# Four image layers in one Trainium2 kernel: layer 0's scores and products in runs of 6, 4, 6 and 4, 8, 4 units

## The chip, the cores and the metric

The kernel runs on one core of a Trainium2 chip. A core has a matrix engine (TensorE, PE in the profile), a vector engine (VectorE, DVE), a scalar engine (ScalarE, ACT), GpSimd (POOL) and DMA queues, of which SyncE (SP) issues most here. They run side by side[...]. The metric is the device time of one execution in microseconds (us); lower is better.

## The reference

The input is four images of 64 x 64 places with 64 channels, in float32. Four layers follow one another:

```python
# layer 0: attention over the N = 4096 places of an image
q, k, v = x @ Wq + bq, x @ Wk + bk, x @ Wv + bv
attn = softmax(q @ k.T, axis=-1)
x = gamma * (attn.T @ v) + x              # summed over the query place
# layer 1: LayerNorm, 64 -> 256, 3x3 depthwise convolution, two halves multiplied,
#          channel attention, 128 -> 64, added to x; LayerNorm, 64 -> 256,
#          two halves multiplied, 128 -> 64, added to x
# layer 2: self-attention between the 64 x 64 rows "b, c" of the image, on x itself
x = softmax(x @ x.T) @ x + x
# layer 3: attention with 32 inner channels, a projection to 64, BatchNorm over all images
f = softmax((x @ theta) @ (x @ phi).T, axis=-1)
wy = (f @ (x @ g)) @ W + b
x = x + batchnorm(wy)
```

In layer 0 the softmax runs over the keys j of a query i, and the product sums over i. So for each tile of 128 queries the kernel makes the scores against all keys, takes their exponential, and scales v of these queries by the reciprocal of the row sums; the product then adds this tile's part to all 4096 outputs.

## The kernel before, in words

**Layout.** `X` keeps the four images in SBUF, each as 128 partitions (two halves of the image by 64 channels) by 2048 places. PSUM is divided into three buffers `ps` of 128 x 1024 (scores, projections and all else) and two accumulators `acc` of 128 x 512. The exponentials go to six buffers `e` of 128 x 2048 in SBUF.

**Layer 0** has 32 tiles t of 128 queries an image. `scores(t)` has four parts g. Each part is four matmuls of 64 x 64 weights (four quarters of the array at once), which fill one `ps`, and one exponential on ScalarE with the row sums in `zs` (lines 1031 and 1036). I call a part a score unit. `scale(t)` on VectorE adds the four sums, takes the reciprocal and multiplies v into `vq` (lines 1045 to 1048). `products(p, half)` takes two tiles, 2p and 2p + 1, and half of the outputs: for each of the two tiles and two accumulators, two matmuls of 128 x 64 weights with `vq` as the weights (line 1056). I call these two matmuls a product unit. An accumulator that has both tiles is added to `y` on VectorE (line 1063). The profile counts each float32 matmul as two.

**The order** is written out by hand: PE, ScalarE and VectorE take their instructions as the program emits them. A list `items` holds one entry for each layer 0 tile (then for the steps of layers 2 and 3), and `due[i]` what comes after item i. Two lanes, `conv` and `misc`, hold generators of other work. The lane of `conv` runs layer 1 of image b beside layer 0 of image b + 1; its longest part is the depthwise convolution, nine taps for each of 4 x 2 blocks, every tap one VectorE instruction of 128 x 1024 (lines 1155 to 1160). The lane of `misc` turns and projects the images to come (`load_x`, `project0`). A generator yields the us that its step is to take, and `tick(us)` lets a lane catch up:

```python
fn()                                   # scores(t)
for lane in (conv, misc):
    lane.tick(us)                      # 3.6
for fn in due.get(i, []):              # products(p, half), then scale(t)
    fn()
for lane in (conv, misc):
    lane.tick(us)
```

So a round is four score units, lane work, four product units, the scale of that round's tile, lane work. In `due` the products were entered ahead of the scales, and products of tiles 2p and 2p + 1 begin in the round of tile 2p + 2.

**Other places that the change touches.** `fetch_x` loads image 0 in two halves; `setup` turns the small vectors and folds LayerNorm into `pw1` and `pw3`, in item 3 (lines 879 to 912); `project0` makes q with its bias on VectorE (line 990) and v; in layer 3, `products` adds exponentials on VectorE into `esum`, and `totals` turns the sums of a block of 32 steps into reciprocals with a logarithm, an exponential and a Newton step; `finish` makes the BatchNorm and stores, with `check_sums` ahead of the last copies.

Of the kernel before, what the change touches and what calls it, by code (L numbers as in the profile page):

```python
# [691 lines left out]
def fast_path(ctx: ExitStack, tc: tile.TileContext, a: dict, out: bass.AP, bad):  # L692
# [44 lines left out]

    def fetch_x(b, queues):
        if b % 2 == 0:
            fetch_x.both = new_big("xr")  # L740
        t = fetch_x.both[:, bass.ts(b % 2, 2048)].rearrange("p (q n) -> p q n", n=128)
        src = a["x"][b].rearrange(by_rows, p=2, q=16)
        for g in range(2):
            for p in range(2):
                (queues[p] if b == 0 else queues[g]).dma_start(
                    out=t[64 * p : 64 * p + 64, bass.ts(g, 8)], in_=src[p, :, bass.ts(g, 8)]
                )
        rows_x.append(t)
# [3 lines left out]
    nc.sync.dma_start(out=qk[:, 64:128], in_=a["L0_conv_Wk"])  # L752
    fetch_x(0, (nc.sync, nc.scalar))
    bq = const.tile([64, 1], F32, name="bq")
    nc.sync.dma_start(out=bq, in_=a["L0_conv_bq"].rearrange("(n o) -> n o", o=1))
# [123 lines left out]
    def setup():  # L879
        nc.vector.tensor_add(cmat, cmat, ident)  # L880
        ps = new_ps()
        nc.tensor.transpose(ps[:, 512 : 512 + n_rows], rows, ident[:n_rows, :n_rows])
        nc.vector.tensor_copy(vec, ps[:, 512 : 512 + n_rows])
        yield 5.0

        ps = new_ps()
        for i, (w_, sh, bi) in enumerate(
            ((pw1, "L1_conv_ln1_b", "L1_conv_pw1_b"), (pw3, "L1_conv_ln2_b", "L1_conv_pw3_b"))
        ):
            for r in range(2):  # L890
                mm(
                    ps[:, 2 * i + r : 2 * i + r + 1], w_[0:64, bass.ts(r, 128)], V(sh, 0, 0, 64),
                    start=True, stop=True,
                )
            nc.vector.tensor_add(
                pwb[:, i, :], ps[:, 2 * i : 2 * i + 2], vec[:, col[bi] : col[bi] + 2]
            )

        ps = new_ps()
        for i, (w_, g) in enumerate(((pw1, "L1_conv_ln1_g"), (pw3, "L1_conv_ln2_g"))):  # L900
            nc.vector.tensor_scalar_mul(w_, w_, V(g))
            mm(ps[:, 512 * i : 512 * i + 256], cmat, w_, start=True, stop=True)
            nc.vector.tensor_copy(w_, ps[:, 512 * i : 512 * i + 256])
        for i in range(4):
            nc.vector.tensor_scalar_mul(half[:, bass.ts(i, 64)], ident[:, 0:64], 0.5)
            stt(
                half[:, bass.ts(i, 64)], ident[:, 64:128], -0.5 if i > 1 else 0.5,
                half[:, bass.ts(i, 64)], ALU.mult, ALU.add,
            )
        nc.vector.tensor_mul(resb[:, 0:1], V("L1_conv_pw2_b"), V("L1_conv_beta"))  # L910
        nc.vector.tensor_mul(resb[:, 1:2], V("L1_conv_pw4_b"), V("L1_conv_gamma"))
        yield 3.0
# [7 lines left out]
    def load_x(b):  # L920
        for g in range(2):
            ps = new_ps()
            for i in range(8):
                nc.tensor.transpose(ps[:, bass.ts(i, 128)], rows_x[b][:, 8 * g + i, :], ident)
            (nc.vector.tensor_copy if g else nc.scalar.copy)(X[:, b, bass.ts(g, 1024)], ps)
            yield 3.0
# [44 lines left out]
    def project0(b):  # L971
# [5 lines left out]
        for j, w in once if b else ((0, "q"), (0, "v"), (1, "q"), (2, "q"), (1, "v"), (3, "q")):  # L977
            ps = new_ps()
            if w == "once":
# [7 lines left out]
                for o in range(2):  # L987
                    own, other = slice(64 * o, 64 * o + 64), slice(64 - 64 * o, 128 - 64 * o)
                    n = bass.ts(2 * j + o, 512)
                    nc.vector.tensor_scalar_add(  # L990
                        qs[own, :, n], ps[own, :].rearrange("p (s n) -> p s n", s=2), bqk[own, :]
# [26 lines left out]
    def layer0(b):  # L1018
        x, m, first = X[:, b], im[b], len(items)
        tiles = {}  # L1020

        def scores(t):
            es = [new_e() for _ in range(2)]
            zs = sm.tile([128, 4], F32, tag="zs", name="zs", bufs=4)
            vq = sm.tile([128, C], F32, tag="vq", name="vq", bufs=4)
            for g in range(4):
                ps = new_ps()
                for c in range(2):
                    for r in range(2):
                        rows_ = slice(64 * r, 64 * r + 64)  # L1030
                        mm(  # L1031
                            ps[64 * c : 64 * c + 64, bass.ts(r, 512)],
                            m.q[rows_, 128 * t + 64 * c : 128 * t + 64 * c + 64],
                            x[rows_, bass.ts(g, 512)], start=True, stop=True,
                        )
                act(  # L1036
                    es[g // 2][:, bass.ts(g % 2, 1024)], ps, AF.Exp, bias=SHIFT0,
                    accum_out=zs[:, g : g + 1],
                )
            tiles[t] = es, vq, zs  # L1040

        def scale(t):
            es, vq, zs = tiles[t]
            tot = sums0[:, b, t : t + 1]
            nc.vector.tensor_reduce(tot, zs, AX.X, ALU.add)
            rec = sm.tile([128, 1], F32, tag="rec", name="rec")
            nc.vector.reciprocal(rec, tot)
            nc.vector.tensor_scalar_mul(vq, m.v[:, t, :], rec)

        def products(p, half):  # L1050
            accs = [new_acc() for _ in range(2)]
            for t in (2 * p, 2 * p + 1):
                es, vq, _ = tiles[t]
                for g in range(2):
                    for r in range(2):
                        mm(  # L1056
                            accs[g][64 * r : 64 * r + 64, :], vq,
                            es[half][:, 1024 * g + 512 * r : 1024 * g + 512 * r + 512],
                            start=t == 2 * p, stop=t == 2 * p + 1,
                        )  # L1060
            for g in range(2):
                cols = bass.ts(2 * half + g, 512)
                stt(  # L1063
                    (x if p == 15 else m.y)[:, cols], accs[g], gam0,
                    (m.y if p else x)[:, cols], ALU.mult, ALU.add,
                )

        for t in range(32):
            items.append((lambda t=t: scores(t), 3.6))
        for p in range(16):  # L1070
            for half in range(2):
                at(first + 2 * p + 2 + half, lambda p=p, half=half: products(p, half))
        for t in range(32):
            at(first + t, lambda t=t: scale(t))
# [156 lines left out]
    def layer2(b):  # L1231
# [51 lines left out]
        for n in range(32):  # L1283
            items.append((lambda n=n: scores(n), 4.6))
            at(first + n + 1, lambda n=n: products(n))
# [3 lines left out]
    def close2(b):  # L1289
# [4 lines left out]
        for i in range(4):  # L1294
# [4 lines left out]
            yield 2.0 if i < 3 else 6.0  # L1299
# [3 lines left out]
    wys, early = {}, []  # L1303

# [44 lines left out]
    def layer3(b):  # L1349
# [3 lines left out]
        def scores(n):  # L1353
# [12 lines left out]
            for kp in range(2):  # L1366
                act(e[:, bass.ts(kp, 1024)], tiles[kp], AF.Exp)  # L1367

        def products(n):
# [4 lines left out]
            if mc % 10 == 9 or (last and n >= 62):  # L1374
# [9 lines left out]
            elif mc:  # L1384
                nc.vector.tensor_add(esum, esum, e)  # L1385
            if last and n == 63:
                sums()
            for k in range(4):
                mm(  # L1389
                    st["y"][32 * k : 32 * k + 32, :], m.gx[:, mc, :], e[:, bass.ts(k, 512)],  # L1390
                    start=mc == 0, stop=mc == 31,
                )
            if mc == 31 and not (last and n == 63):
                st["yz"] = new_t("yz")
                nc.scalar.copy(st["yz"][:, 0:512], st["y"])  # L1395

# [7 lines left out]
        def totals(nb):  # L1404
            sums()
            yz, z = st["yz"], st["z"]

            t = new_t("inv")
            r, d = t[:, 0:512], t[:, 512:1024]
            act(r, z, AF.Ln)  # L1410
            act(r, r, AF.Exp, scale=-1.0)
            nc.vector.tensor_mul(d, z, r)  # L1412
            stt(d, d, -2.0, r, ALU.add, ALU.mult, accum_out=inv3[:, 2 * b + nb : 2 * b + nb + 1])
            stt(yz[:, 0:512], d, -1.0, yz[:, 0:512], ALU.mult, ALU.mult)

# [42 lines left out]
        for n in range(64):  # L1458
# [4 lines left out]
            elif n % 32 == 31:  # L1463
                at(first + n + (2 if n == 63 and b < 2 else 4), lambda n=n: totals(n // 32))
                at(first + n + 8, lambda n=n: close(n // 32))


    conv_from, misc_from, misc_to = {}, {}, {}
    for b in range(B):
        if b:  # L1470
            misc_to[len(items)] = True
        layer0(b)
        if b + 1 < B:
            gens = [load_x(i) for i in range(1, B)] if b == 0 else []
            misc_from[32 * b + 16] = gens + [project0(b + 1)]
        conv_from[32 * b + 34] = layer1(b)
    misc_from[112] = [features2(0)]
# [17 lines left out]
    def run():  # L1495
# [6 lines left out]
        next(loads)  # L1502
        misc.add(first)
        conv_from[3] = setup()
        for i in range(max(max(due) + 1, len(items))):
# [6 lines left out]
            us = 1.0  # L1512
            if i < len(items):
                fn, us = items[i]
                fn()
            for lane in (conv, misc):
                lane.tick(us)
            for fn in due.get(i, []):
                fn()
            for lane in (conv, misc):  # L1520
                lane.tick(us)
# [14 lines left out]
    def finish():  # L1536
# [34 lines left out]
        def store(i, o):  # L1571
            dst = out[i // 2].rearrange(by_rows, p=2, q=16)[:, :, bass.ts(i % 2, 8)]
            if i < E:
                for p in range(2):
                    nc.sync.dma_start(
                        out=dst[p].rearrange("h q n -> h (q n)"), in_=o[64 * p : 64 * p + 64, 0:1024]
                    )
            else:
                nc.sync.dma_start(out=dst.rearrange("p h q n -> h p (q n)"), in_=o[:, 0:1024])
# [42 lines left out]
        for i in range(E, 2 * B):  # L1622
# [5 lines left out]
            else:  # L1628
                check_sums(mv)
                nc.vector.tensor_copy(os[i][:, 0:512], pss[i][:, 0:512])  # L1630
                nc.scalar.copy(os[i][:, 512:1024], pss[i][:, 512:1024])
            store(i, os[i])
# [74 lines left out]
```

## Time and profile before

| what | value |
|---|---|
| device time, median of 3 (lowest to highest) | 2654.57 us (2653.53 to 2654.67) |
| span of the profiled execution | 2652.8 us |
| PE, VectorE, ScalarE busy | 2612.8, 1348.6, 1718.6 us |
| layer 0, first score to last product | 14.4 to 1049.3 us |
| its score matmuls (L1031), product matmuls (L1056) | 475.5, 467.4 us |
| its exponentials (L1036) | 517.1 us |
| depthwise taps of the main form (L1157), all layers | 308.1 us in 240 instructions |

In a line of the grouped view stand: line, engine, operation, output and inputs by name, shapes and count; then busy us and mean ns of one; then the idle time of the engine ahead of them and what ended it. In a line of the timeline stand: start and length in us, engine, line, operation, count, and in brackets the idle time ahead of it and what ended it. A line that merges several instructions has the length from the first start to the last end. In the view of stretches (a range of us, then its length) stand busy us and instructions of PE, PE's weight loads, VectorE, ScalarE and GpSimd; then the granted clock of PE, 1 being full, the share of the DMA engines and GB/s.

### The profile page before, as it was taken

The numbers are of one execution on the slowest core, as the hardware profiler recorded it, in microseconds if no ns is written. First come the engines' busy times: TensorE is split into PE (matmuls) and PEld (weight loads), VectorE is DVE, ScalarE is ACT, GpSimd is POOL, SyncE is SP. The second block draws the span as 40 slices with busy tenths as digits, with TensorE's granted clock in tenths as the row PEclk, the third lists the DMA queues.
The fourth block names the chain that finished last, engine by engine and source line by source line (L and its number), as shares of the span: only waits on it lengthen the run. The fifth ranks groups of instructions, "written<-read, shape, count | busy, mean of one in ns | idle before, by whom it ended". The sixth has DMA issues, their size and how long they took to land.

```text
span 2652.8 us, 50797 instructions
## 1 busy us (share of the span) xinstructions
PE 2612.8 (98%) x22421; PEld 830.2 (31%) x22421; DVE 1348.6 (51%) x1555; ACT 1718.6 (65%) x2787; POOL 16.4 (1%) x66
## 2 busy tenths in 40 slices
PE   8999999999999999999999999999999999999998
PEld 3333233333323323333333322243322333322223
DVE  3232386633876338621672148800068600098997
ACT  4555655656566565666656668756578755578886
POOL 2000000000000000000000000000000000000000
PEclk9999999999999999999999999999999999999999
DMA  3000000001000100010010000010000010010002
GB/s 73 1 17 1 17 8 10 1 17 25 9 1 1 32 17 1 1 33 17 1 33 17 17 1 1 2 33 1 17 1 2 1 33 1 1 33 2 1 1 66
DMA packets 24282, 36.46 MB, mean 14 GB/s; under 512 B 3725, under 2 KB 12150, under 8 KB 24054
## 3 DMA queue, kind: packets, MB, share of 16 engines
q1 hardware_dynamic: 23141, 32.03, 5.5%
q8 instruction: 178, 2.92, 0.5%
q0 software_dynamic: 672, 0.56, 0.1%
q10 hardware_dynamic: 240, 0.54, 0.1%
q14 instruction: 51, 0.41, 0.1%
HBM read 4.80 MB, written 4.19 MB: 3 GB/s over the span
## 4 chain that ended last, share of the span: by engine, by line
PE 93%; DVE 4%; ACT 2%; issue 0%; DMA 0%; SPq 0%; DVEq 0%; ACTq 0%
PE acc L1056 17%; PE acc L1262 17%; PE ps L1031 17%; PE ps L1245 16%; PE ps L1361 10%; PE acc L1389 8%; PE ps L1118 2%; DVE tg L1385 2%; PE accz L1378 1%; ACT e L1253 1%; PE ps L1209 1%; PE ps L1186 1%; PE ps L1088 1%; PE ps L1340 1%; PE ps L1007 0%
## 5 line engine op out<-in xcount | busy, mean ns | idle before, releaser
L1036 ACT ACTIVATE e<-ps 128x1024 f32<-128x1024 f32 x512 | 517.1, 1025 | 338.1 <-PE ps L1031 225.8
L1253 ACT ACTIVATE e<-ps 128x1024 f32<-128x1024 f32 x512 | 517.0, 1025 | 305.0 <-PE ps L1245 304.9
L1367 ACT ACTIVATE e<-ps 128x1024 f32<-128x1024 f32 x512 | 496.0, 1022 | 85.4 <-PE ps L1361 78.3
L1385 DVE TENSOR_TENSOR tg<-tg,e 128x2048 f32<-128x2048 f32 x214 | 490.4, 2292 | 24.7 <-ACT e L1367 5.7
L1031 PE MATMUL ps<-X,q 64*64 64x512 f32 x4096 | 475.5, 599 | 7.6 <-DVE q L990 4.1
L1245 PE MATMUL ps<-ko 64*64 64x512 f32 x4096 | 469.8, 591 | 2.2 <-ACT ko L1227 1.6
L1262 PE MATMUL acc<-e,X 64*64 64x512 f32 x4096 | 468.5, 591 | 2.6 <-DVE inv L1412 1.6
L1056 PE MATMUL acc<-e,vq 128*64 128x512 f32 x2048 | 467.4, 598 | 0.0
L1063 DVE SCALAR_TENSOR_TENSOR yv<-acc,gam,yv 128x512 f32<-128x512 f32 x224 | 167.8, 750 | 322.6 <-PE acc L1056 311.7
L1157 DVE SCALAR_TENSOR_TENSOR y<-pad,vec,y 128x1024 f32<-128x1024 f32 x240 | 308.1, 1284 | 8.1 <-ACT pad L1141 1.0
L1361 PE MATMUL ps<-tg,ph 32*64 32x512 f32 x4096 | 309.5, 613 | 1.4 <-DVE tg L1329 0.5
L1389 PE MATMUL acc<-e,tg 128*32 128x512 f32 x2048 | 272.0, 603 | 1.5 <-ACT yz L1395 1.5
L1245 PEld LDWEIGHTS ps<-ko 64*64 64x64 f32 x4096 | 157.7, 132 | 288.1 <-issue 195.4
L1262 PEld LDWEIGHTS acc<-e,X 64*64 64x64 f32 x4096 | 159.1, 133 | 278.7 <-issue 263.3
L1031 PEld LDWEIGHTS ps<-X,q 64*64 64x64 f32 x4096 | 143.2, 133 | 323.7 <-issue 224.8
L1056 PEld LDWEIGHTS acc<-e,vq 128*64 128x64 f32 x2048 | 136.0, 136 | 315.1 <-issue 294.4
L1270 DVE TENSOR_TENSOR ph<-ph,acc 128x512 f32<-128x512 f32 x16 | 11.0, 688 | 379.6 <-ACT ph L1269 379.6
L1361 PEld LDWEIGHTS ps<-tg,ph 32*64 32x64 f32 x4096 | 79.5, 129 | 218.7 <-issue 143.2
L1389 PEld LDWEIGHTS acc<-e,tg 128*32 128x32 f32 x2048 | 43.5, 108 | 202.3 <-issue 196.3
L1253 ACT ACTIVATION_READ_ACCUMULATOR e<-ps 128x1 f32 x512 | 106.1, 207 | 0.0
L1036 ACT ACTIVATION_READ_ACCUMULATOR e<-ps 128x1 f32 x512 | 106.0, 207 | 0.0
L1141 ACT ACTIVATE pad<-ps,pwb 128x512 f32<-128x512 f32 x64 | 44.6, 697 | 45.7 <-PE ps L1118 39.0
(193 smaller groups left out, 939.9 us busy)
## 6 DMA issues: line engine op xcount, KB each, us to landing
xn<-t SPq DMA_DIRECT2D x64, 128.0 KB
ph<-tg SPq DMA_DIRECT2D x64, 128.0 KB
ko<-ko SPq DMA_DIRECT2D x16, 256.0 KB
xr<-in_x_dram SPq DMA_DIRECT2D x14, 256.0 KB
q<-q SPq DMA_DIRECT2D x12, 256.0 KB
out_dram<-o SPq DMA_DIRECT2D x5, 512.0 KB
out_dram<-o SPq DMA_DIRECT2D x6, 256.0 KB
xr<-in_x_dram ACTq DMA_DIRECT2D x2, 256.0 KB
```

The source lines that it names most:

```text
L1031: mm(ps[64 * c : 64 * c + 64, bass.ts(r, 512)], m.q[rows_, 128 * t + 64 * c : 128 * t + 64 * c + 64], x[rows_, bass.ts(g, 512)], start=Tru ...
L1036: act(es[g // 2][:, bass.ts(g % 2, 1024)], ps, AF.Exp, bias=SHIFT0, accum_out=zs[:, g : g + 1],)
L1056: mm(accs[g][64 * r : 64 * r + 64, :], vq, es[half][:, 1024 * g + 512 * r : 1024 * g + 512 * r + 512], start=t == 2 * p, stop=t == 2 * p + 1,)
L1063: stt((x if p == 15 else m.y)[:, cols], accs[g], gam0, (m.y if p else x)[:, cols], ALU.mult, ALU.add,)
L1157: stt(y1, win, wt, y1, ALU.mult, ALU.add)
L1245: mm(ps[64 * c : 64 * c + 64, bass.ts(r, 512)], m.ko[rows_, 128 * jb + 64 * c : 128 * jb + 64 * c + 64], m.ko[rows_, bass.ts(2 * ib + r, 5 ...
L1253: act(es[n, jb], ps, AF.Exp, bias=SHIFT2, accum_out=m.zs[:, jb, ib : ib + 1])
L1262: mm(acc[r][64 * c : 64 * c + 64, :], xw[rows_, jb, :], es[n, jb][rows_, bass.ts(c, 512)], start=jb == 0, stop=jb == 31,)
L1361: mm(tiles[kp][64 * c : 64 * c + 64, bass.ts(i, 512)], m.ph[rows_, 128 * mc + 64 * c : 128 * mc + 64 * c + 64], m.th[rows_, bass.ts(nb, 51 ...
L1367: act(e[:, bass.ts(kp, 1024)], tiles[kp], AF.Exp)
L1385: nc.vector.tensor_add(esum, esum, e)
L1389: mm(st["y"][32 * k : 32 * k + 32, :], m.gx[:, mc, :], e[:, bass.ts(k, 512)], start=mc == 0, stop=mc == 31,)
```

## The change

The change gives layer 0's score and product units a common order over all four images, in longer runs: scores in runs of 4, 6, 6 and products of 8, 4, 4, alternately, so that six changes between the two kinds stand where eight stood. The lanes get 0.9 us for each unit, ahead of and behind the products separately. A product unit now finishes one accumulator before it opens the next. The q of images 1 to 3 is given its bias on ScalarE. Image 0 comes in three parts, the third of which is turned within the first tile of scores; bq is loaded first, on another queue. `setup` is cut into more steps, with its matmuls together. In layer 3 the work on the sums of a block is spread over several steps, one exponential at a block's start is held back until the copy of the accumulator has been emitted, and the last block sums its last four steps on PE. The last copies are stored half by half, and the checks of the sums follow them.

```diff
+    parts = ((0, 4), (4, 8), (8, 16)), ((0, 8), (8, 16))
...
-        for g in range(2):
+        for lo, hi in parts[b > 0]:
             for p in range(2):
...
+                queues[p].dma_start(out=t[64 * p : 64 * p + 64, lo:hi], in_=src[p, :, lo:hi])
...
+    bq = const.tile([64, 1], F32, name="bq")
+    nc.gpsimd.dma_start(out=bq, in_=a["L0_conv_bq"].rearrange("(n o) -> n o", o=1))
     fetch_x(0, (nc.sync, nc.scalar))
...
+        for w_, g, _, _ in folds:
+            nc.vector.tensor_scalar_mul(w_, w_, V(g))
+        yield 5.0
         ps = new_ps()
...
+        for i, (w_, _, _, _) in enumerate(folds):
             mm(ps[:, 512 * i : 512 * i + 256], cmat, w_, start=True, stop=True)
+        for i, (w_, _, _, _) in enumerate(folds):
             nc.vector.tensor_copy(w_, ps[:, 512 * i : 512 * i + 256])
...
-                    nc.vector.tensor_scalar_add(
-                        qs[own, :, n], ps[own, :].rearrange("p (s n) -> p s n", s=2), bqk[own, :]
+                    act(
+                        qs[own, :, n], ps[own, :].rearrange("p (s n) -> p s n", s=2),
+                        AF.Identity, bias=bqk[own, :],
                     )
...
+    def score0(i):
+        b, t, g = i // 128, i // 4 % 32, i % 4
...
+        if g % 2 == 0:
+            es[g // 2] = new_e()
+        if g == 2 and between:
+            between.pop()()
...
+    def product0(i):
+        b, p, half, g, o = i // 128, i // 8 % 16, i // 4 % 2, i // 2 % 2, i % 2
...
+        if o == 0:
+            m.acc = new_acc()
+        es, vq, _ = tiles[b, 2 * p + o]
...
+    def layers0():
+        n, done, turned = 128 * B, 0, 0
+        ends = [(4, 0), (8, 0)]
+        for m in range(n // 16):
+            ends += [(16 * m + 12, 16 * m + 4), (16 * m + 16, 16 * m + 12), (16 * m + 22, 16 * m + 16)]
+        for i, (s, p) in enumerate(ends):
+            s = min(s, n)
+            if s > done:
+                items.append(
+                    (lambda lo=done, hi=s: [score0(k) for k in range(lo, hi)], (0.9 * (s - done), 0.9 * (p - turned)))
+                )
+                for k in range(done // 4, s // 4):
+                    at(i, lambda k=k: scale0(k // 32, k % 32))
+            if p > turned:
+                at(i, lambda lo=turned, hi=p: [product0(k) for k in range(lo, hi)])
+            done, turned = s, p
...
-            if mc % 10 == 9 or (last and n >= 62):
+            if mc % 10 == 9 or (last and n >= 60):
...
+            if last and n == 62:
+                return
...
+            steps = [
+                lambda: log(slice(0, 256)), lambda: log(slice(256, 512)),
+                lambda: exp(slice(0, 256)), lambda: exp(slice(256, 512)), lambda: newton(n // 32),
+            ]
...
             for lane in (conv, misc):
-                lane.tick(us)
+                lane.tick(us[0])
             for fn in due.get(i, []):
                 fn()
             for lane in (conv, misc):
-                lane.tick(us)
+                lane.tick(us[1])
...
+        i = 2 * B - 1
+        nc.vector.tensor_copy(os[i][:, 0:512], pss[i][:, 0:512])
+        store(i, os[i], 0)
+        nc.scalar.copy(os[i][:, 512:1024], pss[i][:, 512:1024])
+        store(i, os[i], 1)
+        check_sums(mv)
```

## The prediction

> **What bounds the kernel now.** I read the page first (engine shares, chain), then the grouped rows, then the timeline of layer 0 in a quiet stretch and in a stretch with depthwise work, last the waits.
>
> ```profile
> PE 2612.8 (98%) x22421; PEld 830.2 (31%) x22421; DVE 1348.6 (51%) x1555; ACT 1718.6 (65%) x2787; POOL 16.4 (1%) x66
> ...
> PE 93%; DVE 4%; ACT 2%; issue 0%; DMA 0%; SPq 0%; DVEq 0%; ACTq 0%
> ...
> L1031 PE MATMUL ps<-X,q 64*64 64x512 f32 x4096 | 475.5, 599 | 7.6 <-DVE q L990 4.1
> L1056 PE MATMUL acc<-e,vq 128*64 128x512 f32 x2048 | 467.4, 598 | 0.0
> L1063 DVE SCALAR_TENSOR_TENSOR yv<-acc,gam,yv 128x512 f32<-128x512 f32 x224 | 167.8, 750 | 322.6 <-PE acc L1056 311.7
> L1157 DVE SCALAR_TENSOR_TENSOR y<-pad,vec,y 128x1024 f32<-128x1024 f32 x240 | 308.1, 1284 | 8.1 <-ACT pad L1141 1.0
> ```
> TensorE (PE) carries the chain. The averages say that VectorE (DVE) has half its time free; the next views show where that is false. A quiet stretch of layer 0, PE alone:
>
> ```profile
> 303.35 3.66 PE L1031 MATMUL ps<-X,q 64*64 64x512 f32 x32
> 306.94 3.65 PE L1056 MATMUL acc<-e,vq 128*64 128x512 f32 x16
> 310.52 3.66 PE L1031 MATMUL ps<-X,q 64*64 64x512 f32 x32
> ```
> A run of four score units, then one of four product units, 3.585 us from start to start. Inside a run, groups of matmuls start 0.429 us apart (306.40 from 305.97, say), two groups to a unit, so four units need 3.43 us: each change between the 64x64 and the 128x64 tiling costs 0.152 us. Now VectorE while layer 1's depthwise convolution of the previous image runs beside layer 0:
>
> ```profile
> 349.76 1.61 DVE L1063 SCALAR_TENSOR_TENSOR yv<-acc,gam,yv 128x512 f32<-128x512 f32 x2 [0.33 <-PE acc L1056]
> 351.28 0.15 DVE L1045 TENSOR_REDUCE sums<-zs 128x1 f32<-128x4 f32 x1
> 351.46 0.16 DVE L1047 RECIPROCAL rec<-sums 128x1 f32<-128x1 f32 x1
> 351.66 0.26 DVE L1048 TENSOR_SCALAR vq<-yv,rec 128x64 f32<-128x64 f32 x1
> 351.83 5.24 DVE L1157 SCALAR_TENSOR_TENSOR y<-pad,vec,y 128x1024 f32<-128x1024 f32 x4
> 357.01 1.61 DVE L1063 SCALAR_TENSOR_TENSOR yv<-acc,gam,yv 128x512 f32<-128x512 f32 x2
> ```
> VectorE has no free time here: two sums, a scale, four taps, 7.25 us a round, and PE's rounds are 7.2 long. See the order: the scale stands behind the sums of the products, and its vq is read a whole round later. Last, the longest PE wait of layer 0 and the clock after it:
>
> ```profile
> 403.95 1.09 PE L1031 MATMUL ps<-X,q 64*64 64x512 f32 x8 [3.15 <-DVE q L990]
> ...
> 405.30:408.70 3.40, 3.40 (x19) 2.40 (x12) 0.00 (x0) 2.30 (x4) 0.00 (x0) 0.50 0.34 68
> ```
> PE stood 3.15 us behind a q eviction queued on the full VectorE, and then ran 3.4 us at half clock.
>
> [...]
>
> **The change, part by part.** Call 16 score units and 16 product units a period; layer 0 has 32.
>
> 1. *Longer runs.* A period had 8 tiling changes and has 6: 2 x 0.152 = 0.304 us saved. Against it: in a run of six scores, unit u+3 needs the PSUM tile of unit u. From the ScalarE rows of the quiet run (first exp 1.156 us after the run's start, pitch 1.0, release about 1.17 after each exp's start), the sixth unit's weights may load at 4.33 us, where the matmul itself is due at 4.34. There is nothing left to prefetch, and the next group starts 0.48 instead of 0.43 later, as it does at every run's head: 0.05 a run of six, two a period, 0.10. Net -0.20 a period where VectorE is free.
>
> 2. *A new dependence.* Before, products of a pair needed vq scaled one round earlier. Now the run of scores 22 to 27 of a period (then 6 further each time) is followed at once by products 16 to 19, and the second of these, 17, needs vq of tile 5, whose last scores (22, 23) stand in that same run. Its scale is emitted after that run and after the taps that the lane got in `tick(us[0])`. Queued behind product 17 on PE is everything: later products, the next scores.
>  With VectorE free this hides: unit 23's exp is released 3.3 us into the score run, the scale takes 0.55, product 17 is due at 6.2. With taps it does not. A tap costs 1.27 us on average (rows of 1.295 pitch, the cheaper first and split last). From the end of the 8 products, in us: last sum 0.12 to 0.88; 4+3 taps to 9.77; scale to 10.32; two sums (0.76 each) to 11.84; 2+3 taps to 18.19; scale of tile 5 to 18.74. PE meanwhile: 5.36 (six scores) + 3.585 (four products) + 5.36 + 0.91 = 15.22 when product 17 is due. It starts at 18.80: stall 3.6. Going on, the four taps and a scale before the 8 products put their first sum at 28.04 to 28.80, and the third accumulator, of two buffers, is due at 28.6: 0.3 more. The period ends at 32.45.
>  Check by VectorE's own sum: 16 taps 20.3, 8 sums 6.1, 4 scales 2.2, together 28.6, plus idle time waiting for PE of 0.64, 0.96, 1.25 and 0.96 (sums now come one accumulator at a time, 1.72 us apart): 32.4. Before, a period took 28.74 there (342.63 to 371.37 between sums). So +3.71 a period. The taps are paced by units and not by time, so their number of periods stays: two whole images of 64.8 + 72 us of lane time (36 and 40 steps of 1.8) are 9.5 periods, and 48 us of a third fall into layer 0: 11.2. That is +41.6 us. The other 20.8 periods give 20.8 x 0.20 = -4.2.
>
> 3. *Clock.* Each such stall leaves PE empty for about 3 us, close to the 3.15 that was followed by half clock for 3.4 us. One drop can cost at most 1.7. I take half of the 11.2, at 1.0 each, since VectorE is behind anyway: +5.6 (0 to 19).
>
> 4. *q eviction to ScalarE.* The stalls between score groups that belong to q or to its queue sum to some 7.5 us, and the half clock to 1.7: 9.2 removed. Added: two 64x1024 Identity of about 1.1 us (ScalarE's L1203, 128x1024, is 1.125), six times; where they stand just ahead of a score run the third unit waits some 0.8 and the rest keep ScalarE's pace, about 1.4 for half of the six or 0.7 mean, so about 4. Net -5.
>
> 5. *Pads.* The pad evictions (0.70 each, two a step) ahead of a run of six make more units keep ScalarE's 1.0 pace instead of 0.857: today 0.09 to 0.14 a step, then up to 0.45, and two steps may come together: +4.
>
> 6. *Setup.* Today PE stands or trickles from 45.6 to 50.6 and runs at half clock to 53.7. Matmuls are issued together and the VectorE halves come a lane step earlier; about 3 us of the 6.6 stay: -3.6.
>
> 7. *First loads.* Scores start at 14.43. A quarter image can be turned and projected earlier, and bq (landed 10.1 today) no longer waits behind x; the third part's turn and 1.23 us copy now stand between the second and third unit and give most back: -1.5.
>
> 8. *Layer 3 block ends:* the waits there are 0.5 to 1.0 us each, ten of them, 5 in all; split logs and exps and a held exp hide part: -2. *Last sums and stores:* a stall of 0.55 ahead of the last sums, and the last copies stand 0.75 behind the flag's checks: -1.3.
>
> Sum: 41.6 - 4.2 + 5.6 - 5 + 4 - 3.6 - 1.5 - 2 - 1.3 = +33.6; 2654.6 becomes 2688.
>
> **Rivals.**
> A. The tap lag does not bind (VectorE gets ahead of PE in ways that my queue misses). Then depthwise periods go to 28.45, -0.29 each, -3.2; with -4.2, -13.4 from parts 4, 6, 7, 8 and +4: -16.8, so 2638. For it: VectorE is only 51% busy and PE never waited for a scale before. Against: that free time is not in these stretches, and the scale had a round of slack that is gone.
> B. Only the 5 taps directly ahead count, without the backlog of the 7: last sum to 0.88 after PE's four products, taps to 7.2, scale to 7.8, product due at 6.2: a stall of 1.7, period 30.2, +1.46 x 11.2 = 16.4, no clock loss; +2.8 in all, 2657, no change. Against: total VectorE work of 28.6 leaves nothing to catch up with.
> C. Every stall drops the clock: 19 in place of 5.6, 2702.
>
> **How the numbers follow.** My forecast 0.50, A 0.23, B 0.10, C 0.17. Faster takes A and a little of B: 0.25; no change 0.08; slower 0.67. The range runs from A's upper half to just past C, 2640 to 2706.
>
> **What would show it.** Right: in the profile after, within depthwise stretches, L1056-type products wait 3 to 4 us for the vq scale about once in 32 us, 11 times, VectorE shows idle time before sums there, and layer 0 is some 35 us longer; half clock appears in several of these places. Elsewhere PE's layer 0 shows 6 changes a period and the q waits are gone. Wrong: no PE wait on vq, or layer 0 shorter than before; then the queue order that I read from the emission is not what binds. If waits on ScalarE's exps dominate instead, part 1 or 5 was too small.

## The result, and the profile after

| | before | after |
|---|---|---|
| device time, median (lowest to highest) | 2654.05 us (2653.16 to 2654.67) | 2696.80 us (2693.69 to 2701.21) |
| ratio, 95% interval | | 1.0163 [1.0145, 1.018] |
| layer 0, start of the first score to end of the last product (traces) | 14.4 to 1049.9 us: 1035.5 | 10.1 to 1089.4 us: 1079.3 |
| from there to the end | 1602.9 us | 1602.4 us |

The changed kernel is 43 us slower; 2688 was predicted, in a range of 2640 to 2706. The traced execution of the changed kernel took 2693.69 us, the least of its four, so the trace shows 39 of these 43 us: layer 0 starts 4.3 us earlier and lasts 43.8 us longer, and what follows takes 0.5 us less. The other three, 2695.61 to 2701.21 us, had a mean granted clock of 0.996 to 0.994, where the traced one had 0.997; they have no trace, so what they lost beyond it is not shown.

Below are the engines and some groups of instructions of the kernel after. The line numbers have moved: scores are L1048, products L1070, the sums of products L1077, the three instructions of a scale L1058, L1060 and L1061.

```profile
PE 2618.0 (97%) x22429; PEld 814.0 (30%) x22429; DVE 1334.7 (50%) x1542; ACT 1726.6 (64%) x2814; POOL 17.1 (1%) x67
...
L1070 PE MATMUL acc<-e,vq 128*64 128x512 f32 x2048 | 470.5, 603 | 34.6 <-DVE sums L1058 24.7
...
L1048 PE MATMUL ps<-X,q 64*64 64x512 f32 x4096 | 473.5, 599 | 7.4 <-ACT e L1053 2.7
...
L1077 DVE SCALAR_TENSOR_TENSOR yv<-acc,gam,yv 128x512 f32<-128x512 f32 x224 | 167.2, 749 | 151.5 <-PE acc L1070 151.2
L1058 DVE TENSOR_REDUCE sums<-zs 128x1 f32<-128x4 f32 x128 | 19.5, 153 | 195.8 <-ACT e L1053 195.8
```

No engine works more than before to speak of. What is new stands in the last columns: the products, ahead of which PE had been idle for 0.0 us, now have 34.6 us of idle time ahead of them, and VectorE has 195.8 us ahead of the scales, where a scale blocks its queue until the last exponential of a run is done. Before, the first instruction of a scale had no idle time ahead of it:

```profile
L1045 DVE TENSOR_REDUCE sums<-zs 128x1 f32<-128x4 f32 x128 | 18.8, 147 | 0.0
```

The waits of PE in the kernel after (us in total, times, longest) show what nearly all of that 34.6 is made of, in the first two of these lines:

```profile
PE acc L1070 <- DVE sums L1058: 24.7, 14, 3.1
PE acc L1070 <- DVE vq L1061: 9.7, 5, 3.2
PE ps L1111 <- ACT sq L1105: 5.3, 3, 1.9
PE ps L1268 <- ACT pad L1164: 3.6, 3, 2.2
```

The first two lines are one thing. The view names the VectorE instruction that ended last before PE went on. Two scales stand one behind the other there, and where the second one's first instruction (L1058) was through as PE started, it is named in place of the vq of the first. Here is one such place in a depthwise stretch, PE and then VectorE in the timeline:

```profile
369.52 5.48 PE L1048 MATMUL ps<-X,q 64*64 64x512 f32 x48
374.93 1.08 PE L1070 MATMUL acc<-e,vq 128*64 128x512 f32 x4
379.19 2.79 PE L1070 MATMUL acc<-e,vq 128*64 128x512 f32 x12 [3.18 <-DVE vq L1061]
...
371.89 5.24 DVE L1180 SCALAR_TENSOR_TENSOR y<-pad,vec,y 128x1024 f32<-128x1024 f32 x4
377.16 1.42 DVE L1183 SCALAR_TENSOR_TENSOR yg<-pad,vec,y 128x512 f32<-128x512 f32 x2
378.49 0.15 DVE L1058 TENSOR_REDUCE sums<-zs 128x1 f32<-128x4 f32 x1
378.68 0.17 DVE L1060 RECIPROCAL rec<-sums 128x1 f32<-128x1 f32 x1
378.88 0.26 DVE L1061 TENSOR_SCALAR vq<-yv,rec 128x64 f32<-128x64 f32 x1
379.05 0.15 DVE L1058 TENSOR_REDUCE sums<-zs 128x1 f32<-128x4 f32 x1
379.23 0.16 DVE L1060 RECIPROCAL rec<-sums 128x1 f32<-128x1 f32 x1
379.43 0.25 DVE L1061 TENSOR_SCALAR vq<-yv,rec 128x64 f32<-128x64 f32 x1
380.32 0.75 DVE L1077 SCALAR_TENSOR_TENSOR yv<-acc,gam,yv 128x512 f32<-128x512 f32 x1 [0.63 <-PE acc L1070]
382.03 0.75 DVE L1077 SCALAR_TENSOR_TENSOR yv<-acc,gam,yv 128x512 f32<-128x512 f32 x1 [0.97 <-PE acc L1070]
```

PE does six score units and one product unit (the four matmuls of 374.93) and stops at the second, as predicted: VectorE does five taps (6.6 us) and then the scale, 3.35 us behind the moment at which the unit was due (a run's third group follows 0.91 after its first: 375.84). Then VectorE, full until now, stands idle 0.63 and 0.97 us for the sums; 0.64 and 0.96 had been worked out.

### The profile page after: what moved, and what is told of

Read it like the earlier page. It is cut to its first block, busy times and chain, and to the rows that moved or that the text cites. A ratio compares the mean times of both kernels' runs of the same rounds, so it can differ in the third digit from the quotient of the medians.

```text
span 2691.8 us, 50833 instructions
## 1 busy us (share of the span) xinstructions
PE 2618.0 (97%) x22429; PEld 814.0 (30%) x22429; DVE 1334.7 (50%) x1542; ACT 1726.6 (64%) x2814; POOL 17.1 (1%) x67
## 4 chain that ended last, share of the span: by engine, by line
PE 61%; DVE 3%; ACT 1%; DMA 0%; issue 0%; POOL 0%; SPq 0%; POOLq 0%; DVEq 0%; ACTq 0%
PE acc L1285 16%; PE ps L1268 15%; PE ps L1386 11%; PE acc L1421 9%; PE acc L1070 2%; DVE y L1180 2%; PE ps L1048 1%; PE ps L1141 1%; PE accz L1407 1%; PE ps L1365 1%; ACT e L1053 0%; PE ps L1232 0%; PE ps L1209 0%; PE ps L1111 0%; PE accz L1433 0%; ACT e L1276 0%
## 5 line engine op out<-in xcount | busy, mean ns | idle before, releaser
L1053 ACT ACTIVATE e<-ps 128x1024 f32<-128x1024 f32 x512 | 516.0, 1029 | 333.0 <-PE ps L1048 256.6
L1276 ACT ACTIVATE e<-ps 128x1024 f32<-128x1024 f32 x512 | 516.7, 1025 | 300.0 <-PE ps L1268 300.0
L1070 PE MATMUL acc<-e,vq 128*64 128x512 f32 x2048 | 470.5, 603 | 34.6 <-DVE sums L1058 24.7
L1048 PE MATMUL ps<-X,q 64*64 64x512 f32 x4096 | 473.5, 599 | 7.4 <-ACT e L1053 2.7
L1391 ACT ACTIVATE e<-ps 128x1024 f32<-128x1024 f32 x256 | 262.6, 1026 | 84.5 <-PE ps L1386 70.4
L1180 DVE SCALAR_TENSOR_TENSOR y<-pad,vec,y 128x1024 f32<-128x1024 f32 x240 | 308.1, 1284 | 13.0 <-ACT pad L1164 5.5
L1392 ACT ACTIVATE e<-ps 128x1024 f32<-128x1024 f32 x256 | 261.6, 1022 | 0.0
L1070 PEld LDWEIGHTS acc<-e,vq 128*64 128x64 f32 x2048 | 137.4, 137 | 352.7 <-issue 257.4
L1077 DVE SCALAR_TENSOR_TENSOR yv<-acc,gam,yv 128x512 f32<-128x512 f32 x224 | 167.2, 749 | 151.5 <-PE acc L1070 151.2
L1268 PEld LDWEIGHTS ps<-ko 64*64 64x64 f32 x4096 | 151.9, 132 | 297.2 <-issue 202.6
L1048 PEld LDWEIGHTS ps<-X,q 64*64 64x64 f32 x4096 | 138.2, 132 | 329.6 <-issue 166.7
L1285 PEld LDWEIGHTS acc<-e,X 64*64 64x64 f32 x4096 | 153.3, 133 | 278.3 <-issue 277.0
L1058 DVE TENSOR_REDUCE sums<-zs 128x1 f32<-128x4 f32 x128 | 19.5, 153 | 195.8 <-ACT e L1053 195.8
```

Source lines behind the costliest of these rows:

```text
L1048: mm(ps[64 * c : 64 * c + 64, bass.ts(r, 512)], m.q[rows_, 128 * t + 64 * c : 128 * t + 64 * c + 64], x[rows_, bass.ts(g, 512)], start=Tru ...
L1053: act(es[g // 2][:, bass.ts(g % 2, 1024)], ps, AF.Exp, bias=SHIFT0, accum_out=zs[:, g : g + 1])
L1070: mm(m.acc[64 * r : 64 * r + 64, :], vq, es[half][:, 1024 * g + 512 * r : 1024 * g + 512 * r + 512], start=o == 0, stop=o == 1,)
L1180: stt(y1, win, wt, y1, ALU.mult, ALU.add)
L1268: mm(ps[64 * c : 64 * c + 64, bass.ts(r, 512)], m.ko[rows_, 128 * jb + 64 * c : 128 * jb + 64 * c + 64], m.ko[rows_, bass.ts(2 * ib + r, 5 ...
L1276: act(es[n, jb], ps, AF.Exp, bias=SHIFT2, accum_out=m.zs[:, jb, ib : ib + 1])
```

## The experiments

All are timed against the kernel before, which took 2653.9 to 2654.2 us beside them.

**1. Rounds of four, all other edits kept.**

```diff
-        ends = [(4, 0), (8, 0)]
-        for m in range(n // 16):
-            ends += [(16 * m + 12, 16 * m + 4), (16 * m + 16, 16 * m + 12), (16 * m + 22, 16 * m + 16)]
+        ends = [(4 * k + 4, max(4 * k - 4, 0)) for k in range(n // 4 + 2)]
...
-                for k in range(done // 4, s // 4):
-                    at(i, lambda k=k: scale0(k // 32, k % 32))
             if p > turned:
                 at(i, lambda lo=turned, hi=p: [product0(k) for k in range(lo, hi)])
+            for k in range(done // 4, s // 4):
+                at(i, lambda k=k: scale0(k // 32, k % 32))
...
```

The lines left out give the lanes 3.6 us on both sides of each round's products and set the items at which lane work starts to those of the rounds.

> The changed kernel, with layer 0 back in rounds of four score units and four product units, each scale behind the products and used a round later; all its other edits stay. Theory (a vq that is used right behind the scores it comes from): PE no longer waits for a scale, layer 0 falls from 1079 us to about 1033, the kernel to about 2643 (2635 to 2650), below the kernel before. Rival (the q eviction on ScalarE, the setup or the other edits carry the loss): it stays above 2680.

Measured: 2637.24 us, ratio 0.9934 [0.9917, 0.995]. Layer 0 takes 1029.5 us, and no PE wait on a scale is left. Its end, 1595.9 us from layer 0's last product, is 6.5 shorter than in the changed kernel. So the loss comes with the runs; the other edits gain 17 us together.

**2. The runs alone, in the kernel before.** `layer0` and the two `tick` calls are as in the change, and the items at which lane work starts are set to match; nothing else is changed.

```diff
-    def layer0(b):
...
+    def score0(i):
...
+    def layers0():
...
-                lane.tick(us)
+                lane.tick(us[0])
```

> The kernel before, with the new order of layer 0's units alone (runs of 6, 4, 6 and 4, 8, 4, the scale ahead of the products, the lanes' us split); loads, setup, q on VectorE, layer 3 and the end as before. Theory: the loss is all here, 2700 (2690 to 2715), with some 35 us of PE waits on the scale. Rival (the other edits carry the loss): below 2665.

Measured: 2718.17 us, ratio 1.024 [1.0223, 1.0257]: 64 us are lost by the runs alone. That is the expected sign, and 3 us above the range that was expected. PE's waits on the scale:

```profile
PE acc L1056 <- DVE vq L1047: 19.4, 9, 3.2
PE acc L1056 <- DVE sums L1044: 16.3, 10, 3.0
```

They add up to 35.7 us, as expected. The traced execution had a mean granted clock of 0.993, where those of the changed kernel and of the kernel before had 0.997. The difference, 0.004 of its 2714 us, is some 11 us; by this estimate a lower clock can be a part of the rest.

**3 and 4. Lighter taps, in both kernels.** The 240 taps of the main form work on one column of sixteen, so most of the convolution is left out; in experiment 3 they take 68.1 us in place of 308.1.

```diff
                     elif k < 8 or not r:
-                        stt(y1, win, wt, y1, ALU.mult, ALU.add)
+                        stt(y1[:, 0:1], win[:, 0:1], wt, y1[:, 0:1], ALU.mult, ALU.add)
```

> The changed kernel; of the nine depthwise taps those from the second to the eighth (and the ninth of the second half) work on one image column of sixteen, so about 15 of 16 parts of that work are left out and VectorE is mostly free in these stretches. Theory: the waits of products on the scale inside the depthwise stretches (27 us) and the clock drops there vanish, those outside (12 us) stay: about 2664 (2655 to 2672). Rival (VectorE's load doesn't matter, the scale waits for the exponentials[...]): above 2685.

> The kernel before with the same work of the depthwise taps left out. Theory: it has a round of slack for the scale, so it hardly moves: 2648 (2642 to 2654), from the q waits on a full VectorE. Rival (the taps cost the kernel before as much as the changed one): below 2635.

Measured: the changed kernel falls by 37 us to 2659.88 (ratio to before 1.0022 [1.0013, 1.003]), the kernel before by 3 to 2651.00 (0.9988 [0.9981, 0.9995]). The same work, taken out of VectorE, is worth some twelve times as much where a vq stands behind it that is needed at once. What is left of the waits in the changed kernel:

```profile
PE acc L1070 <- DVE sums L1058: 6.6, 6, 1.8
...
PE acc L1070 <- DVE vq L1061: 5.0, 3, 2.0
```

These are nine waits, at the same steps as in the changed kernel (at 152.5 us, 284.2 and so on). Eight lie outside the depthwise stretches, the ninth near the beginning of one (at 681.2 us). The taps explain the other ten waits of the changed kernel, all within the stretches or at their end, and not these nine.

**5. The scale ahead of the taps.** A scale whose tile is complete before the last unit of its run is emitted behind the scores, ahead of `tick(us[0])`.

```diff
-                    (lambda lo=done, hi=s: [score0(k) for k in range(lo, hi)], (0.9 * (s - done), 0.9 * (p - turned)))
+                    (
+                        lambda lo=done, hi=s: [score0(k) for k in range(lo, hi)]
+                        + [scale0(k // 32, k % 32) for k in range(lo // 4, hi // 4) if 4 * k + 4 < hi],
+                        (0.9 * (s - done), 0.9 * (p - turned)),
+                    )
...
                 for k in range(done // 4, s // 4):
-                    at(i, lambda k=k: scale0(k // 32, k % 32))
+                    if 4 * k + 4 == s:
+                        at(i, lambda k=k: scale0(k // 32, k % 32))
```

> The changed kernel; a scale whose tile is complete before the last score of its run is emitted straight behind these scores, ahead of the lanes' taps, the others as in the change. Theory (the taps queued ahead of the scale): the wait for the scale inside the depthwise stretches goes, though VectorE still loses time waiting for sums there: about 2670 (2655 to 2682), waits of PE on the scale below 12 us. Rival (the scale waits for its exponentials): no faster than 2690.

Measured: 2659.12 us (1.0018 [1.001, 1.0027]): 38 us of the changed kernel's loss undone by the place of one small instruction group in one queue. No wait on a scale is left, and another comes into view, 7.0 us for an accumulator that VectorE hasn't taken yet (L1077):

```profile
PE acc L1070 <- DVE yv L1077: 7.0, 8, 1.3
```

**6 and 7. Runs of 4, 8, 4 scores**, so that the tile in question is complete a run earlier; then also with lane time in the middle of the 8 products.

```diff
-            ends += [(16 * m + 12, 16 * m + 4), (16 * m + 16, 16 * m + 12), (16 * m + 22, 16 * m + 16)]
+            ends += [(16 * m + 12, 16 * m + 4), (16 * m + 16, 16 * m + 12), (16 * m + 24, 16 * m + 16)]
```

```diff
-                    (lambda lo=done, hi=s: [score0(k) for k in range(lo, hi)], (0.9 * (s - done), 0.9 * (p - turned)))
+                    (lambda lo=done, hi=s: [score0(k) for k in range(lo, hi)], (0.9 * (s - done), 3.6 if p > turned else 0.0))
...
-                at(i, lambda lo=turned, hi=p: [product0(k) for k in range(lo, hi)])
+                at(i, lambda lo=turned: [product0(k) for k in range(lo, lo + 4)])
+                if p - turned == 8:
+                    at(i, lambda: [lane.tick(3.6) for lane in (conv, misc)])
+                    at(i, lambda lo=turned: [product0(k) for k in range(lo + 4, lo + 8)])
```

> The changed kernel with score runs of 4, 8, 4 in place of 4, 6, 6, so that the tile whose vq was needed at once is now complete a whole run earlier; as many changes of tiling as in the change. Theory (the missing slack): PE waits on the scale nearly vanish, VectorE's waits for sums in the run of 8 products stay: 2655 (2643 to 2668). Rival (long runs cost in themselves, by ScalarE's pace in a run of eight): above 2680.

> As the runs of 4, 8, 4, and the lanes get their time also in the middle of the run of 8 products, so that taps fill VectorE between its sums. Theory: 2634 (2628 to 2644), at or below the rounds of four with the other edits (2637). Rival (no gain is left in fewer tiling changes): 2645 or above.

Measured: 2657.55 us (1.0013 [1.0006, 1.002]), then 2644.24 us (0.9964 [0.995, 0.9978]). With the slack alone, the waits on the scale are gone and the one on the accumulators is there again; PE and VectorE in a run of 8 products of the first of the two:

```profile
446.31 3.65 PE L1070 MATMUL acc<-e,vq 128*64 128x512 f32 x16
...
450.53 1.41 DVE L1077 SCALAR_TENSOR_TENSOR yv<-acc,gam,yv 128x512 f32<-128x512 f32 x2
451.33 3.65 PE L1070 MATMUL acc<-e,vq 128*64 128x512 f32 x16 [1.37 <-DVE yv L1077]
453.31 0.75 DVE L1077 SCALAR_TENSOR_TENSOR yv<-acc,gam,yv 128x512 f32<-128x512 f32 x1 [1.38 <-PE acc L1070]
```

Both accumulators were full at 450, while VectorE worked through taps and a scale; the fifth product unit waited 1.37 us for the first of them, and VectorE then 1.38 us for the third. With lane time in the middle of that run this wait is gone and 13 us are won. At 2644.24 the expected range (up to 2644) is missed at its edge, and the kernel is 7 us behind the rounds of four: in this version no gain is left in fewer changes of tiling. In a quiet stretch, a period (between starts of product runs) takes 28.71 us before (62.88 to 91.59), 28.54 in the change (70.18 to 98.72) and 28.74 here (69.14 to 97.88, by its trace): a run of eight scores gives back all that two changes save.

**8. Rounds of four, the scale ahead of the round's products**, still used a round later: the two blocks of the `due` entries of experiment 1 in the change's order.

> The changed kernel in rounds of four and four, as before, but with the scale ahead of the round's products, as the change has it; the vq is still used a round later. Theory (the round of slack decides, not the place in the queue): 2637, within 5 us. Rival (a scale ahead of the sums holds VectorE up): 2650 or above.

Measured: 2636.92 us (0.9936 [0.9919, 0.9952]), the same as with the scale behind (2637.24). The place of the scale made no difference here, where its reader comes a round later.

**9. Rounds of four, q back on VectorE.**

```diff
-                    act(
-                        qs[own, :, n], ps[own, :].rearrange("p (s n) -> p s n", s=2),
-                        AF.Identity, bias=bqk[own, :],
-                    )
+                    nc.vector.tensor_scalar_add(
+                        qs[own, :, n], ps[own, :].rearrange("p (s n) -> p s n", s=2), bqk[own, :]
+                    )
```

> The changed kernel in rounds of four and four (2637), with the q of images 1 to 3 given its bias on VectorE again, as before. Prediction's part 4: its move to ScalarE is worth 5 us, so 2642 (2638 to 2647), with PE waits on q of some 4 us and a clock drop back. Rival (it is hidden either way): within 1.5 us of 2637.

Measured: 2641.63 us (0.9955 [0.9942, 0.9969]), 4.4 above experiment 1. Whether a drop of the clock is back is not shown by the mean granted clock, 0.998 in the traced execution as in that of experiment 1. The wait is back:

```profile
PE ps L1047 <- DVE q L999: 4.1, 2, 3.1
```

**10. The change's own runs with both mends**, those of experiments 5 and 7.

> The changed kernel's runs of 6, 4, 6 and 4, 8, 4 with both mends: a scale whose tile is complete before its run ends stands ahead of the taps, and the lanes get time in the middle of the run of 8 products. Theory (the loss is queue order on VectorE, not the runs): no PE waits on the scale or on sums, 2637 (2630 to 2644), no worse than the rounds of four. Rival (long runs cost elsewhere, by lane work that waits behind six exponentials on ScalarE): 2646 or above.

Measured: 2649.58 us (0.9979 [0.9972, 0.9987]). Here the theory was missed and the time is that of the rival: 4.6 us below the kernel before and 47 below the change, and still 12 behind the rounds of four. By the traces 7.7 of these 12 us lie in layer 0 (1037.15 against 1029.47) and 4.8 behind it (1600.67 against 1595.88). In layer 0 PE is idle for 7.4 us more than in the rounds of four: waits of 4.8 us for accumulators are new, and waits of 3.7 us, at two places, of lane work that stands behind six exponentials; others have become shorter. PE and ScalarE at one of these two places:

```profile
276.29 1.06 PE L1119 MATMUL ps<-X,jsel 128*32 128x512 f32 x8
...
277.01 1.05 ACT L1053 ACTIVATE e<-ps 128x1024 f32<-128x1024 f32 x1
...
278.01 2.03 ACT L1113 ACTIVATE sq<-X 128x1024 f32<-128x1024 f32 x2
...
279.15 2.87 PE L1119 MATMUL ps<-sq,jsel 128*32 128x512 f32 x8 [1.80 <-ACT sq L1113]
```

The squares of LayerNorm start when the sixth exponential is through, and PE, whose queue already holds the matmul that reads them, stands 1.8 us. The 2.87 us for 8 matmuls, where the line above has 1.06, are in part the wait for the second square. PE was also slower for a time: the four product matmuls that follow, at 281.94, took 1.44 us, where four took 1.08 in the changed kernel (at 374.93). What makes the 4.8 us behind layer 0 was not taken apart.

## Why the prediction was right, point by point

**The mechanism** is the one that was put first. The unit named (product 17, and one like it in each period), the five taps ahead of the scale, and VectorE's idle times after it are in the trace as worked out. Experiments 1 and 2 place the loss in the runs; 3 and 4 place the greater part in the taps; 5 and 8 show that it takes both, a scale behind the taps and a reader right behind the run.

**The term of 41.6 us** was near in its sum and wrong in its place. By the matmuls' starts, PE's delays between products in layer 0 of the changed kernel come to 27.0 us in the depthwise stretches and 12.5 outside, 39.5 in all. Within the stretches, eleven long waits of 1.0 to 3.35 us have a mean of 2.3 (25.7 / 11), where 3.6 was taken for each; four are above 3 us. So the number of places was right, and their size was taken too large. From unit 17 of one period to unit 17 of the next, five periods with depthwise work (from 346.98, 452.43, 730.00, 794.59 and 826.43 us) take 30.9 to 33.1 us, 31.8 in the mean; the same five took 28.7 to 28.8 before. That is +3.1 where +3.71 was worked out, the drop of the clock at 452.70 included. Outside the stretches nothing was priced. That too much within and nothing outside nearly cancel is luck. One place outside, VectorE and then ScalarE and PE:

```profile
953.73 1.28 DVE L1228 SCALAR_TENSOR_TENSOR u<-ps,pwb,t 128x1024 f32<-128x1024 f32 x1 [0.36 <-PE ps L1141]
961.35 0.69 DVE L1235 TENSOR_TENSOR X<-X,t 128x512 f32<-128x512 f32 x1 [6.34 <-ACT t L1233]
961.96 1.21 DVE L1250 COPY ko<-ps 64x1024 f32<-64x1024 f32 x1
963.10 0.14 DVE L1058 TENSOR_REDUCE sums<-zs 128x1 f32<-128x4 f32 x1
...
959.51 1.05 ACT L1053 ACTIVATE e<-ps 128x1024 f32<-128x1024 f32 x1
...
960.51 0.81 ACT L1233 ACTIVATE t<-ps,resb,vec 128x512 f32<-128x512 f32 x1
...
963.78 4.49 PE L1070 MATMUL acc<-e,vq 128*64 128x512 f32 x12 [1.95 <-DVE sums L1058]
```

VectorE isn't full here, it is blocked: an addition of layer 1 waits 6.34 us for a ScalarE result that stands behind six exponentials, and the scale stands behind the addition and a copy. The queue that was read for work should have been read for waits as well. That is the step that fell short, and experiment 3 shows it: with the taps' work gone, these waits remain.

**The other terms.** *Runs*: -0.20 us a period predicted, -0.17 measured in the quiet stretch. *Clock*: +5.6 predicted; the traced execution has three drops within layer 0, 3.41 us each at 0.50 of the clock, so at most 1.7 each and up to 5.1 by this estimate. *q on ScalarE*: -5 predicted, -4.4 in the rounds of four, by experiments 1 and 9. *Setup*: -3.6 predicted; the round that holds it was 6.45 us too long (42.07 to 55.70, against 7.18) and is 2.04 too long in experiment 1 (40.42 to 49.64), so -4.4. *First loads*: -1.5 predicted; the first score starts 4.3 us earlier, but PE then waits 1.41 us for the third part's copy (at 15.33 us in experiment 1), and the round that holds the setup's first matmuls starts at 40.42 us in experiment 1 against 42.07 before: -1.65, so the third part gives back most of it, as predicted. *Layer 3 and the end*: -3.3 predicted; experiment 1 shows -7.0 for all that follows layer 0 (1602.9 to 1595.9), the changed kernel only -0.5. There, lane work falls on other steps of layer 2, where waits on the pads (3.6 us) are new. PE's idle time behind layer 0 is 2.4 us longer than in experiment 1, so such waits are a part of the difference of 6.5, and the rest of it is open. *Pads*, +4, was not measured by itself. Near it stands what the prediction has no term for: in layer 0 of the changed kernel PE waits 3.7 us for squares (at 280.3 and 992.0), 2.0 for a normalised input (at 569.1) and 2.7 for exponentials, 8.4 in all against 0.4 before. With these 8.0, and -5.4 for the runs (0.17 in each of 32 periods), the terms as measured add up to some 36 of the 39 us of the traced execution: 39.5 + 8.0 + 5.1 - 5.4 - 4.4 - 4.4 - 1.65 - 0.5.

Of the rivals, A (the lag doesn't bind, 2638) fell, as the lag binds. Experiment 1's 2637 lies close to its number, but has no long runs; with the long runs kept and the lag taken out, experiment 10 gives 2650, so they cost more than A allowed. B and C fell too: the stalls are neither 1.7 us each nor all followed by a drop.

What carried the forecast is that VectorE does its instructions in the order in which they are emitted. These runs show it: in the depthwise stretch of the changed kernel the scale starts at 378.49 us, behind the five taps emitted ahead of it (371.89 on), though PE's product was due at 375.84; and in experiment 5, where the scale was emitted ahead of the taps, 38 us went.

## What to carry to other kernels

When instructions are regrouped into longer runs, list for every reader in which run its operand is made, and what is queued ahead of that on the engine that makes it: work, and instructions that themselves wait. A share of 51% busy says nothing of a stretch in which the engine is full (7.25 us of work in rounds of 7.2), and a producer that has lost its round of slack turns that stretch's backlog into the other engine's waits. Price the gain first: six instead of eight changes of tiling were worth 0.17 us in 28.7, by that some 5 us in all 32 periods of layer 0, and one late operand of 3 us a period outweighs it many times; the fastest version here is the change without its runs, 2637 us, 17 below the kernel before.

## What the runs showed of the hardware that had not been expected

The length of one idle time did not tell whether the clock drops. In the changed kernel delays of 3.35, 3.25 and 3.22 us (at 379, 826 and 1069 us) were followed by no drop, while those of 3.25, 2.55 and 2.12 us (at 452, 486 and 964) were; in experiment 10 PE was slower behind a wait of 1.80 us (at 279.15).

Where the idle time falls tells more in this trace. Every drop but the one at the end of the run lasted 3.41 us, whatever the wait had been, and the three of layer 0 began at 452.70, 486.83 and 964.70 us: 34.13 and 477.87 us apart, which is 10 and 140 times 3.413. So layer 0 is divided here into stretches of that length, counted from the first drop. The view, first for the two stretches that share the delay at 379, then for those just ahead of the three drops, and last for the first drop itself:

```profile
374.20:377.61 3.41, 1.81 (x12) 0.20 (x4) 3.30 (x4) 2.67 (x6) 0.00 (x0) 1.00 0.00 0
377.61:381.02 3.41, 1.83 (x10) 0.69 (x12) 2.64 (x9) 0.00 (x0) 0.00 (x0) 1.00 0.00 0
449.29:452.70 3.41, 0.33 (x4) 0.20 (x4) 3.24 (x8) 0.92 (x2) 0.00 (x0) 1.00 0.00 0
483.42:486.83 3.41, 1.30 (x6) 0.48 (x8) 2.64 (x12) 0.59 (x2) 0.00 (x0) 1.00 0.01 2
961.29:964.70 3.41, 1.46 (x10) 0.35 (x8) 2.78 (x8) 1.04 (x2) 0.00 (x0) 1.00 0.05 11
452.70:456.10 3.40, 3.40 (x10) 0.98 (x8) 0.97 (x2) 0.00 (x0) 0.00 (x0) 0.50 0.00 0
```

The delay at 452 lies almost whole in one stretch, which is left with 0.33 us of PE work, and the clock drops; the delay at 379 is divided between two, both keep 1.8 us, and it does not. In layer 0 of this trace the three stretches ahead of the drops are those with the least PE work (0.33, 1.30 and 1.46 us); the next has 1.54 (988.60 to 992.01). No sharp limit comes out: in the kernel before, with stretches counted from its drop at 405.28 us, one with 1.70 us of PE work (46.88 to 50.29) was followed by a clock of 0.50 for 3.41 us. What decides is not shown; these are five drops in two traces.
